# Order of VectorE's masks and evictions in a two-layer graph attention kernel

One layer of graph convolution and one of masked attention run over 32 graphs on one core. The change reorders work: in each full period one softmax mask goes behind an eviction of q; the first period gets a matmul piece between two scores, a later place for the combinations of one weight, another order of its statistics, and other banks for turning h; the last period inverts its softmax sums ahead of an eviction.

## The chip, the core and the metric

The kernel runs on one core of a Trainium2 chip. The core has TensorE (PE in the profile: matmuls and transposes, into PSUM), VectorE (DVE), ScalarE (ACT), GpSimd (POOL), SyncE (SP, which issues transfers here) and DMA engines. [...] The metric is the device time of a whole execution in microseconds (us).

## The reference, cut to what matters

```python
def layer0(x, adj, W, b):            # x: (32, 512, 512) f32, adj: (512, 512) of 0 and 1
    Wi, Wj = W[:, :512], W[:, 512:]
    a, deg = adj.astype(x.dtype), adj.sum(axis=1)
    return deg[None, :, None] * (x @ Wi.T + b) + einsum('ij,bjo->bio', a, x @ Wj.T)

def layer1(h, adj, Wq, bq, Wk, bk, Wv, bv, Wo, bo):       # 8 heads of 64
    q, k, v = split_heads(h @ Wq.T + bq), split_heads(h @ Wk.T + bk), split_heads(h @ Wv.T + bv)
    scores = where(adj == 0, -inf, q @ k^T / 8)
    return merge_heads(softmax(scores) @ v) @ Wo.T + bo

x = layernorm(x + layer0(x, adj, ...))
x = layernorm(x + layer1(x, adj, ...))
```

## The kernel before

The kernel is one software pipeline over the graphs. In period n the attention of graph n-1 (scores, exponential, mask, values, sums) is interleaved with the projections of graph n and, from n = 2, with the output projection of graph n-2. Period 0 has no attention yet, period 1 has no output projection yet, and the last one (32) has no next graph.

Each 512x512x512 product is done in seven products of half the size in each dimension ("pieces" 1 to 7) with sums and differences of quarters, which GpSimd forms for the activations (`combos`) and which are formed once for the weights (`combine`). A piece is 8 matmuls of 128x128 by 256 columns (16 in layer 0, "l0", which has two products). Pieces of one group share a PSUM bank and accumulate in it; there are two such banks, `mma` and `mmb`, which swap roles from one graph to the next.

```python
GROUP = {1: "X", 2: "X", 6: "Y", 7: "Y", 4: "Y", 5: "Z", 3: "Z"}
ORDER = (1, 2, 6, 7, 4, 5, 3)
LATE = (5, 3, 6, 7, 4)

def piece(kind, b, i, bank):
    ...                                             # cut: which quarters; weights come through a ring of transfers
            nc.tensor.matmul(pm[:, c * Q:(c + 1) * Q], lhs, rhs, start=first, stop=..., skip_group_check=True)   # L436
    prefetch()
    if i == 1:
        nc.scalar.copy(p1, pm)                      # L443
    if kind in ("l0", "pj"):
        ...                                         # cut: i == 1 adds p1 on GpSimd (L451)
            nc.vector.tensor_tensor(d, d, pm, op=OP.add)                         # L454
    else:
        ...                                         # cut: v is evicted on L463 and L465
        if i != 2 and not new:
            nc.vector.tensor_tensor(d, pm, d, op=OP.add)                         # L474
            return
        for c in range(2):
            if i == 2:
                nc.scalar.activation(d[:, c], pm[:, c, :], AF.Identity, bias=bc, scale=1.0)
            else:                                   # q's and k's eviction, with bias and p1: L481
                nc.vector.scalar_tensor_tensor(d[:, c], pm[:, c, :], bc, p1[:, c, :], op0=OP.add, op1=OP.add)
```

The attention of a pair of heads: the scores of 128 keys go to one of two `sc` tiles (two banks each), ScalarE takes the exponential in place, VectorE multiplies by the 0/1 mask into an `e` tile, TensorE forms the values and, at the end of a group g of four heads, the sums. `rest` inverts the sums and scales the values.

```python
def scores(b, hp, kc):
    ps = sc_tile()
    for s in range(2):
        nc.tensor.matmul(ps[:, s, :], KT[...], QT[...], start=True, stop=True)    # L490
    nc.scalar.activation(ps, ps, AF.Exp, scale=QSCALE)                            # L494
def mask(hp, kc):
    nc.vector.tensor_tensor(e, ps, edge[...], op=OP.mult)                         # L499
def presum(i, kc):            # kc == 1: GpSimd, L505; kc > 1: VectorE, L507
def values(b, g, kc):         # TensorE into two ov banks, L516
def sums(g, ...):             # TensorE into an sc tile, L526
def drain(b, g):              # ScalarE, L531
def rest(b, g):               # invert x4 (L535), scale x2 (L544), tell (L539), all VectorE
    return [(invert, g, c) for c in range(4)] + [(scale, b, g, 0), (scale, b, g, 1), (tell, b, g)]
```

Layer norm: `stats` measures two 128-row tiles on VectorE (L298, L299) and has three small steps on GpSimd (L300 to L302), `apply` normalizes them on ScalarE (L305). From graph 2 on, h is turned by a trip through memory; in the first periods TensorE turns it (`l0_norm`).

```python
def l0_norm(b, ic):
    y = XT[b][:, ic, :]
    if ic == 0:
        HT[b] = big()
    pt = turn_tile()                                # an sc tile
    for dc in range(DC):
        nc.tensor.transpose(pt[:, dc * P:(dc + 1) * P], y[:, dc * P:(dc + 1) * P], ident)               # L362
    nc.scalar.copy(HT[b][:, :, ic * P:(ic + 1) * P], pt.rearrange("p (c i) -> p c i", c=DC))            # L363
```

The list of a period's work (phases b and c of graph n, then phase a of graph n+1) is cut into steps by its matmul time. The main loop weaves it into the attention, two steps at a time (`size`), one at a time in the last period (`alone`):

```python
for step in range(0, STEPS, size):
    g, kc = divmod(step, NC)
    extra = []
    for i in range(2):
        scores(b, 2 * g + i, kc)
    for f in due:
        values(*f)
    for i in range(2):
        mask(2 * g + i, kc)
    ...
    if due and due[-1][2] == NC - 1:
        ...
        sums(...); drain(pb, pg)
        extra = rest(pb, pg)
    ...
    if alone:
        ...
    else:
        for i in range(2):
            scores(b, 2 * g + i, kc + 1)
        ...
        late = [(mask, 2 * g + i, kc + 1) for i in range(2)] + extra[-1:] + [f for f in late if f[2] > kc]
        for f in extra[:-1] if extra else late[:1]:
            f[0](*f[1:])
        late, extra = late[0 if extra else 1:], []
    for f in todo:                                  # the pieces of this step, and what goes with them
        ...
        run(f)
        some = 0 if f[0] == 0.0 else ... max(1, round(f[0] / PC))
        ...
        if some:                                    # behind a piece: one late operation
            for g in late[:1] + extra[:some]:
                g[0](*g[1:])
            late, extra = late[1:], extra[some:]
    for g in late + extra:
        g[0](*g[1:])
```

The work of period 1 comes from the first branches of `phase_b` and `phase_c`, which are in the diff below. `combine` for wo is five VectorE operations of 128x512 between SBUF tiles (L261 to L263, L269, L270) and seven stores.

Of the kernel before, what the change touches and what calls it, by code (L numbers as in the profile page):

```python
# [25 lines left out]
def gnn_attention_kernel(  # L26
# [36 lines left out]
    nc = tc.nc  # L63
    B, N, D = x.shape
    NC = N // P
# [17 lines left out]
    def big():  # L83
        return work([P, 4, N], "big", 6)

    def mm_tile(bank):
        return psum.tile([P, 512], FT, name="mm" + bank, bufs=1)
# [4 lines left out]
    def sc_tile():  # L92
        return psum.tile([P, 2, N], FT, name="sc", bufs=2)

    def turn_tile():


        return sc_tile()[:, 0, :]
# [4 lines left out]
    TX, TA, TH, TO = {}, {}, {}, {}  # L103
# [56 lines left out]
    def load_wo():  # L160
        t = work([P, NC, D], "xh", 3)
        for h in range(4):
            for g in range(2):
                nc.sync.dma_start(t[32 * h:32 * h + 32, 2 * g:2 * g + 2], woT.rearrange("(g h r d) o -> g h d r o", g=2, h=4, r=2)[g, h])
        return t

    wo = load_wo()
# [185 lines left out]
            y = XT[b][:, ic, :]  # L353
            nc.vector.scalar_tensor_tensor(y, b0_r, deg_c[:, ic:ic + 1], y, op0=OP.mult, op1=OP.add)

    def l0_norm(b, ic):
        y = XT[b][:, ic, :]
        if ic == 0:
            HT[b] = big()
        pt = turn_tile()  # L360
        for dc in range(DC):
            nc.tensor.transpose(pt[:, dc * P:(dc + 1) * P], y[:, dc * P:(dc + 1) * P], ident)  # L362
        nc.scalar.copy(HT[b][:, :, ic * P:(ic + 1) * P], pt.rearrange("p (c i) -> p c i", c=DC))  # L363
# [26 lines left out]
    def quarter(src, j, n):  # L390
        return src[:, 2 * j:2 * j + 2, Q * n:Q * n + Q]
# [104 lines left out]
    def mask(hp, kc):  # L496
        ps = SC.pop(hp)
        e = E[hp % 2, kc] = work([P, 2, N], "e", 4)
        nc.vector.tensor_tensor(e, ps, edge[:, kc:kc + 1, :].to_broadcast([P, 2, N]), op=OP.mult)  # L499
# [28 lines left out]
    def drain(b, g):  # L528

        j = 2 * (b * 2 + g)  # L530
        nc.scalar.activation(RL[g][1], RL[g][0], AF.Identity, accum_out=told[:, j:j + 1])  # L531
# [22 lines left out]
    PC, TR, GA = 1.73, 0.44, 1.9  # L554
    FLUSH = (0.0, None)

    def z(f, *a):
        return (0.0, f, *a)

    def pc(kind, b, i, bank):  # L560
        return (2 * PC if kind == "l0" else PC, piece, kind, b, i, bank)
# [5 lines left out]
    def banks(n):  # L567

        return ("a", "b") if n % 2 == 0 else ("b", "a")
# [46 lines left out]
    def project(m, i):  # L616

        res = [pc("pj", m, i, banks(m)[1])]
        if i == 1:
            res = [z(combos, TO, m, ot_quarter(m), (1,))] + res  # L620
        if i == 2:
            res = [FLUSH] + res + [z(combos, TO, m, ot_quarter(m), (2, 3, 4))]
        return res

    def phase_b(n):

        m = n - 2
        if m < 0:
            res = []
            side = [z(add_bo, 0, i) for i in range(2)]  # L630
            A, K = banks(n)
            for i, bank in ((2, A), (6, K), (5, A), (7, K), (4, K), (3, A)):
                res.append(pc("l0", n, i, bank))
                if i == 4:
                    res += [z(stats, n, 0)]
                if i in (2, 6):
                    res += [z(combine, "wo", nc.vector, int(i == 6))]
                res += side[:1]
                side = side[1:]
            return res + [z(apply, n, 0), z(stats, n, 1), (TR, l0_norm, n, 0), (TR, l0_norm, n, 1)]  # L640
        A = banks(n)[0]
        l0 = {i: pc("l0", n, i, A) for i in ORDER}
        return [l0[2], *project(m, 1), l0[6], *project(m, 2), l0[7], z(add_bo, n - 1, 0), *project(m, 6), l0[4], z(stats, n, 0),
                *project(m, 7), z(between, apply, n, 0), z(between, h_store, n, 0), z(h_load, n, 0), l0[5], z(add_bo, n - 1, 1), *project(m, 4),
                z(h_turn, n, 0), l0[3], z(stats, n, 1), *project(m, 5)]

    def phase_c(n):

        m = n - 2
        norm = [(TR, l0_norm, n, ic) for ic in range(NC)]  # L650
        h = lambda j, i: quarter(HT[n], j, i)
        A, K = banks(n)
        v, q, k = [{i: pc(kind, n, i, bank) for i in ORDER} for kind, bank in (("v", A), ("q", K), ("k", A))]
        if m < 0:
            res = [v[1]] + ([z(apply, n, 1)] if n else []) + [q[1], v[2], norm[2], norm[3], z(combos, TH, n, h, (1, 2)), k[1],
                                                             z(combos, TH, n, h, (3, 4)), q[2], k[2]]
        else:
            res = [v[1], *project(m, 3), z(apply, n, 1), z(h_store, n, 1), z(stats, m, 0), v[2], z(stats, m, 1),
                   q[1], z(h_load, n, 1), k[1], z(apply, m, 0), q[2], z(between, h_turn, n, 1), z(apply, m, 1), z(store, m),
                   z(combos, TH, n, h, (1, 2)), z(combos, TH, n, h, (3, 4)), k[2]]  # L660
        side = []
        if n == 0:

            side = [z(graph_forms, 2), None, z(graph_forms, 0), None, z(graph_forms, 1)]
        for i in LATE:
            for f in q[i], v[i]:
                res += [f] + [g for g in side[:1] if g]
                side = side[1:]
                if i in (6, 7) and n < B - 1:
                    res += [z(load_xa, n + 1, 2 * (i == 7) + (f is v[i]))]  # L670
            if i == 3 and 0 < n < B - 1:
                res += [z(load_x, n + 1)]
            if i == 7 and n + 1 < B:
                res += [z(ahead, n + 1)]
        return res
# [37 lines left out]
    def run(f):  # L713
        f[1](*f[2:])
# [42 lines left out]
    for n in range(1, B):  # L757
        todo = phase_b(n) + phase_c(n) + phase_a(n + 1)
# [16 lines left out]
    due = []  # L775
    for n in range(1, B + 1):
        b = n - 1

        alone = b == B - 1
        size = 1 if alone else 2  # L780
# [9 lines that stand above are left out]
            todo = [f for todo in PERIODS[n][step:step + size] for f in todo]  # L790
            while todo and todo[0][1] is between:
                run(todo.pop(0))
            if due and due[-1][2] == NC - 1:
                pb, pg = due[-1][:2]
                sums(pg, *(((1, 3), 3) if pb == B - 1 else ()))
                drain(pb, pg)
                extra = rest(pb, pg)
            due = [(b, g, kc + i) for i in range(size)]
            late = [(presum, i, c) for _, _, c in due if c > 0 for i in range(2)]
            if alone:  # L800
                if kc > 2 - g:

                    late = []
            else:
                for i in range(2):
                    scores(b, 2 * g + i, kc + 1)
                for f in late if kc > 0 else []:

                    if f[2] == kc:
                        f[0](*f[1:])  # L810
                late = [(mask, 2 * g + i, kc + 1) for i in range(2)] + extra[-1:] + [f for f in late if f[2] > kc]

                for f in extra[:-1] if extra else late[:1]:
                    f[0](*f[1:])
                late, extra = late[0 if extra else 1:], []
            for f in todo:
                if f is FLUSH:
                    some = len(extra)
                else:
                    if f[1] is l0_norm:  # L820

                        for g in late:
                            g[0](*g[1:])
                        late = []
                    run(f)

                    some = 0 if f[0] == 0.0 else len(extra) if step == 0 and alone else max(1, round(f[0] / PC))
                    if f[1] is piece and f[2] == "l0" and f[4] == 3:

                        some = 0  # L830
                if some:
                    for g in late[:1] + extra[:some]:
                        g[0](*g[1:])
# [3 lines that stand above are left out]
# [21 lines left out]
    with tc.If(flag > 0), tc.tile_pool(name="general", bufs=1) as pools.work:  # L858
        wi, wj, wv, wq, wk, wo = [load_w(work([P, DC, D], f"w{i}", 1), src, nc.sync)
                                  for i, src in enumerate((wiT, wjT, wvT, wqT, wkT, woT))]  # L860
# [28 lines left out]
        with tc.For_i(0, B, 1) as b:  # L889
            g = "general"  # L890
# [21 lines left out]
            for hp in range(HP):  # L912
# [6 lines left out]
                for qb in range(NC):  # L919
# [16 lines left out]
                    for s in range(2):  # L936
                        nc.vector.tensor_scalar(pr[:, s, :], pr[:, s, :], sm[:, 6 + s:7 + s], None, op0=OP.mult)
                        pt = mm_tile("b")
# [57 lines left out]
```

## Time and profile before

| | |
|---|---|
| device time, median of 3 (lowest, highest) | 3677.21 us (3675.18, 3678.22) |
| span of the profiled execution | 3673.2 us, 49737 instructions |
| mean granted TensorE clock | 0.999 |
| TensorE matmuls | 3632.5 us busy, 99% of the span |
| TensorE weight loads (overlapping) | 2519.6 us, 69% |
| VectorE, GpSimd, ScalarE | 2375.0, 2005.7, 1034.5 us busy (65%, 55%, 28%) |
| transfers | 530.02 MB, mean 144 GB/s |
| q's and k's eviction (L481), one of two halves | about 0.476 us |
| a mask (L499) | 1.218 us |

How to read it: a busy time is the share of the span in which an engine has an instruction under way. A wait is idle time of an engine just before an instruction, put down to the instruction that released it. In timeline rows the columns are start, duration, engine, line, operation, output and inputs, the number of like instructions merged in the row, and in square brackets idle time before it with its releaser. The rows of TensorE (PE) overlap a little[...].

### The profile page before, as it was taken

The page shows a single profiled execution, that of the slowest core. Times are in us where ns is not written, and L with a number is a line of the kernel's source. Part 1 is how long each engine was busy: PE and PEld are TensorE (multiplying, and loading weights), DVE is VectorE, ACT ScalarE, POOL GpSimd, SP SyncE. Part 2 cuts the span into 40 slices and gives each one's busy share as a digit, 9 for nine tenths or more (in the row PEclk, how much of TensorE's full clock was granted, in tenths as well). Part 3 has the DMA queues.
Part 4 walks back from the last instruction along what each step waited for, and adds up shares of the span by engine and source line. Part 5 has one row for each costly group of instructions (what it writes and reads, how often), then busy time and mean ns, then how long its engine had stood idle before and what let it go on. Part 6 is the DMA issues. An engine that isn't in the chain of part 4 may idle for free.

```text
span 3673.2 us, 49737 instructions
## 1 busy us (share of the span) xinstructions
PE 3632.5 (99%) x18470; PEld 2519.6 (69%) x18470; DVE 2375.0 (65%) x3133; ACT 1034.5 (28%) x1485; POOL 2005.7 (55%) x1984
## 2 busy tenths in 40 slices
PE   9999999999999999999999999999999999999998
PEld 6666776677667766776677677767776777677663
DVE  4666665666666667666666666666666666666665
ACT  2222222222322223222222232232222322222322
POOL 3556545556446564465654565644656445565443
PEclk9999999999999999999999999999999999999999
DMA  8444555455554555655455545555454555455541
GB/s 258 124 126 134 145 160 151 128 144 146 153 158 135 139 137 145 162 152 132 133 148 157 158 123 143 144 149 161 139 139 137 146 158 153 129 140 145 158 133 52
DMA packets 797174, 530.02 MB, mean 144 GB/s; under 512 B 530432, under 2 KB 611840, under 8 KB 796928
## 3 DMA queue, kind: packets, MB, share of 16 engines
q1 hardware_dynamic: 780384, 494.78, 49.9%
q10 hardware_dynamic: 16320, 31.46, 2.4%
q8 instruction: 150, 2.46, 0.3%
q14 instruction: 96, 0.79, 0.1%
q0 software_dynamic: 224, 0.53, 0.0%
HBM read 453.25 MB, written 73.40 MB: 143 GB/s over the span
## 4 chain that ended last, share of the span: by engine, by line
PE 79%; DVE 8%; DMA 2%; issue 1%; POOL 1%; SPq 1%; ACT 0%; DVEq 0%; POOLq 0%
PE mmb L436 26%; PE mma L436 26%; PE sc L490 11%; PE ov L516 10%; PE mmb L334 3%; PE mma L334 3%; DVE rl L535 3%; DVE e L499 2%; DVE oT L544 1%; DMA xa<-hd 1%; DMA hd<-xh 1%; DVE big L382 1%; PE sc L526 1%; DVE q L481 1%; SPq L376 1%
## 5 line engine op out<-in xcount | busy, mean ns | idle before, releaser
L499 DVE TENSOR_TENSOR e<-sc,edge 128x1024 f32<-128x1024 f32 x512 | 607.7, 1218 | 493.2 <-PE ov L516 479.5
L494 ACT ACTIVATE sc<-sc 128x1024 f32<-128x1024 f32 x512 | 494.5, 1007 | 949.5 <-PE sc L490 937.8
L436 PE MATMUL mmb<-ring,big 128*128 128x256 f32 x3144 | 728.4, 380 | 0.0
L436 PE MATMUL mma<-ring,big 128*128 128x256 f32 x3112 | 721.4, 380 | 3.2 <-DVE xh L454 2.5
L436 PEld LDWEIGHTS mmb<-ring,big 128*128 128x128 f32 x3144 | 593.1, 190 | 105.6 <-issue 24.3
L436 PEld LDWEIGHTS mma<-ring,big 128*128 128x128 f32 x3112 | 586.8, 190 | 109.3 <-issue 23.3
L405 POOL TENSOR_TENSOR big<-big 128x512 f32<-128x512 f32 x376 | 489.2, 1327 | 251.3 <-PE sc L490 234.4
L490 PE MATMUL sc<-q,k 64*128 64x512 f32 x2048 | 513.0, 619 | 2.1 <-DVE e L499 2.0
L204 POOL TENSOR_TENSOR xlo<-xh,xhi 128x512 fp32r<-128x512 f32 x128 | 162.3, 1278 | 570.7 <-ACT xhi L203 570.7
L516 PE MATMUL ov<-e,v 128*32 128x512 f32 x4096 | 468.5, 597 | 2.9 <-DVE oT L544 2.9
L436 PE MATMUL mma<-big,ring 128*128 128x256 f32 x1808 | 430.5, 381 | 6.2 <-DVE q L481 5.3
L436 PE MATMUL mmb<-big,ring 128*128 128x256 f32 x1776 | 422.8, 381 | 6.6 <-DVE q L481 5.0
L436 PEld LDWEIGHTS mma<-big,ring 128*128 128x128 f32 x1808 | 340.2, 190 | 72.6 <-issue 14.1
L436 PEld LDWEIGHTS mmb<-big,ring 128*128 128x128 f32 x1776 | 334.3, 190 | 71.4 <-issue 12.2
L490 PEld LDWEIGHTS sc<-q,k 64*128 64x128 f32 x2048 | 165.5, 185 | 287.0 <-DVE e L499 146.2
L300 POOL TENSOR_SCALAR mv<-mv 128x1 f32<-128x1 f32 x256 | 79.8, 312 | 515.8 <-DVE mv L299 503.5
L516 PEld LDWEIGHTS ov<-e,v 128*32 128x32 f32 x4096 | 119.9, 110 | 330.9 <-issue 325.8
L505 POOL TENSOR_TENSOR es<-e 128x1024 f32<-128x1024 f32 x128 | 300.8, 2361 | 51.2 <-DVE e L499 51.2
L507 DVE TENSOR_TENSOR es<-es,e 128x1024 f32<-128x1024 f32 x250 | 300.8, 1224 | 0.0
L451 POOL TENSOR_TENSOR xh<-xh,p 128x512 f32<-128x512 f32 x186 | 230.6, 1268 | 110.3 <-ACT p L443 110.3
L349 POOL TENSOR_TENSOR big<-big,deg_r 128x512 f32<-128x512 f32 x124 | 212.2, 1711 | 76.4 <-DVE big L348 76.4
L454 DVE TENSOR_TENSOR xh<-xh,mmb 128x512 f32<-128x512 f32 x186 | 127.0, 683 | 192.0 <-PE mmb L436 175.2
(157 smaller groups left out, 3549.8 us busy)
## 6 DMA issues: line engine op xcount, KB each, us to landing
ring<-wo SPq DMA_DIRECT2D x217, 256.0 KB, 2.9
ring<-wq SPq DMA_DIRECT2D x160, 256.0 KB, 3.7
ring<-wv SPq DMA_DIRECT2D x160, 256.0 KB, 3.0
ring<-wk SPq DMA_DIRECT2D x160, 256.0 KB, 4.4
ring<-wi SPq DMA_DIRECT2D x155, 256.0 KB, 2.7
ring<-wj SPq DMA_DIRECT2D x155, 256.0 KB, 2.7
xh<-in_x_dram SPq DMA_DIRECT2D x32, 1024.0 KB, 5.5
xa<-in_x_dram SPq DMA_DIRECT2D x124, 256.0 KB, 4.5
```

The costliest lines, as they stand in the source:

```text
L204: nc.gpsimd.tensor_sub(lo, xs, hi.bitcast(FT))
L334: nc.tensor.matmul(pm, parts[w][:, jc, :], adjR[:, jc, :], start=(w == 0 and jc == 0), stop=(w == 1 and jc == NC - 1))
L349: nc.gpsimd.tensor_tensor(XD[b][:, dc, :], XD[b][:, dc, :], deg_r, op=OP.mult)
L405: nc.gpsimd.tensor_tensor(dst, p, q, op=OP.subtract)
L436: nc.tensor.matmul(pm[:, c * Q:(c + 1) * Q], lhs, rhs, start=first, stop=(kc == 1 and n == len(terms) - 1), skip_group_check=True)
L451: nc.gpsimd.tensor_tensor(d, d, p1, op=OP.add)
L490: nc.tensor.matmul(ps[:, s, :], KT[b, hp // 2][r, hp % 2, kc * P:(kc + 1) * P], QT[b, hp // 2][r, hp % 2, :], start=True, stop=True)
L494: nc.scalar.activation(ps, ps, AF.Exp, scale=QSCALE)
L499: nc.vector.tensor_tensor(e, ps, edge[:, kc:kc + 1, :].to_broadcast([P, 2, N]), op=OP.mult)
L505: nc.gpsimd.tensor_add(ES[i], E[i, 0], E[i, 1])
L507: nc.vector.tensor_add(ES[i], ES[i], E[i, kc])
L516: nc.tensor.matmul(PV[g][r][32 * h:32 * h + 32, :], V[b][:, kc, c0:c0 + 32], E[h // 2, kc][:, h % 2, :], start=(kc == 0), stop=(kc == NC - 1))
```

## The change

In every full period the step at which the second group of heads begins (g = 1, kc = 0) now leaves out the late operation behind its first piece, so that the mask that stood there goes behind the second piece, and so behind q's eviction. In the first attention step of all, where there are no values yet to form, a piece is run between the two pairs of scores. Period 1 takes its l0 pieces in another order, measures the second half of the rows first, turns the first half of h in the banks of the pieces rather than in those of the scores, and moves wo's combinations behind pieces of k and q. In the last period, the inversions of the first group's sums are run as soon as the sums are drained, ahead of the next piece.

```diff
-    def l0_norm(b, ic):
+    def l0_norm(b, ic, bank=None):
...
-        pt = turn_tile()
+        pt = mm_tile(bank) if bank else turn_tile()
...
@@ phase_b, period 1
-            for i, bank in ((2, A), (6, K), (5, A), (7, K), (4, K), (3, A)):
+            for i, bank in ((2, A), (6, K), (5, A), (7, K), (3, A), (4, K)):
                 res.append(pc("l0", n, i, bank))
-                if i == 4:
-                    res += [z(stats, n, 0)]
-                if i in (2, 6):
-                    res += [z(combine, "wo", nc.vector, int(i == 6))]
+                if i == 3:
+                    res += [z(stats, n, 1)]
                 res += side[:1]
                 side = side[1:]
-            return res + [z(apply, n, 0), z(stats, n, 1), (TR, l0_norm, n, 0), (TR, l0_norm, n, 1)]
+            return res + [z(apply, n, 1), z(stats, n, 0), z(apply, n, 0), (TR, l0_norm, n, 0, A), (TR, l0_norm, n, 1, K)]
@@ phase_c, periods 0 and 1
-            res = [v[1]] + ([z(apply, n, 1)] if n else []) + [q[1], v[2], norm[2], norm[3], z(combos, TH, n, h, (1, 2)), k[1],
-                                                             z(combos, TH, n, h, (3, 4)), q[2], k[2]]
+            wo = [z(combine, "wo", nc.vector, i) for i in range(2)] if n == 1 else []
+            res = [v[1], q[1], v[2], norm[2], norm[3], z(combos, TH, n, h, (1, 2)), k[1], *wo[:1], z(combos, TH, n, h, (3, 4)), q[2], *wo[1:], k[2]]
@@ main loop, behind the first pair of masks
+            if not due:
+
+                run(todo.pop(0))
@@ last period
+                if g == 1 and kc == 0:
+
+                    for f in extra[:-1]:
+                        f[0](*f[1:])
+                    extra = extra[-1:]
+                hold = False
@@ full periods
-                late, extra = late[0 if extra else 1:], []
+                late, extra, hold = late[0 if extra else 1:], [], bool(extra) and g == 1
             for f in todo:
...
-                    if f[1] is l0_norm:
-
-                        for g in late:
-                            g[0](*g[1:])
-                        late = []
                     run(f)
...
+                    if some and hold:
+
+                        some, hold = 0, False
                 if some:
                     for g in late[:1] + extra[:some]:
```

More of the change, by code (lines that the diff above doesn't have):

```diff
@@ L649, in phase_c @@
         m = n - 2
-        norm = [(TR, l0_norm, n, ic) for ic in range(NC)]
         h = lambda j, i: quarter(HT[n], j, i)
         A, K = banks(n)
+        norm = {ic: (TR, l0_norm, n, ic) for ic in (2, 3)}
         v, q, k = [{i: pc(kind, n, i, bank) for i in ORDER} for kind, bank in (("v", A), ("q", K), ("k", A))]
         if m < 0:
-            res = [v[1]] + ([z(apply, n, 1)] if n else []) + [q[1], v[2], norm[2], norm[3], z(combos, TH, n, h, (1, 2)), k[1],
-                                                             z(combos, TH, n, h, (3, 4)), q[2], k[2]]
+            wo = [z(combine, "wo", nc.vector, i) for i in range(2)] if n == 1 else []
+            res = [v[1], q[1], v[2], norm[2], norm[3], z(combos, TH, n, h, (1, 2)), k[1], *wo[:1], z(combos, TH, n, h, (3, 4)), q[2], *wo[1:], k[2]]
         else:
```

## The prediction

> **What bounds the kernel now.** I read the busy line of the page first, then TensorE's own waits, then the timeline around each kind of wait. From the page:
>
> ```profile
> PE 3632.5 (99%) x18470; PEld 2519.6 (69%) x18470; DVE 2375.0 (65%) x3133; ACT 1034.5 (28%) x1485; POOL 2005.7 (55%) x1984
> ```
>
> TensorE is busy for 3632.5 of the span's 3673.2 us, so at most 40.7 us of idle time are there to be won, 1.1%. The change removes no matmul. It is therefore about TensorE's waits, listed here as waiting line, releaser, total us, times, longest us:
>
> ```profile
> PE mma L436 <- DVE q L481: 5.3, 15, 0.4
> PE mmb L436 <- DVE q L481: 5.0, 14, 0.4
> PE ov L516 <- DVE oT L544: 2.9, 1, 2.9
> PE mma L436 <- DVE xh L454: 2.5, 2, 1.2
> PE sc L362 <- DVE e L499: 2.4, 1, 2.4
> PE sc L490 <- DVE e L499: 2.0, 2, 1.5
> ...
> PE mma L436 <- issue: 0.9, 1, 0.9
> ```
>
> The first two rows are one small wait in nearly every one of the 30 full periods n = 2 to 31; the others occur once or twice, at the start or the end. The timeline of one such period (start us, us, engine, line, ...):
>
> ```profile
> 509.53 1.29 DVE L544 TENSOR_TENSOR oT<-ov,rl 128x512 f32<-128x512 f32 x2
> ...
> 510.55 1.89 PE L436 MATMUL mma<-ring,big 128*128 128x256 f32 x8
> 510.74 1.22 DVE L499 TENSOR_TENSOR e<-sc,edge 128x1024 f32<-128x1024 f32 x1
> ...
> 511.87 0.87 DVE L481 SCALAR_TENSOR_TENSOR q<-mmb,bq_c,p 128x256 f32<-128x256 f32 x2
> ...
> 512.65 1.22 DVE L499 TENSOR_TENSOR e<-sc,edge 128x1024 f32<-128x1024 f32 x1
> 512.79 1.99 PE L436 MATMUL mmb<-big,ring 128*128 128x256 f32 x8 [0.35 <-DVE q L481]
> ...
> 514.62 1.89 PE L436 MATMUL mma<-ring,big 128*128 128x256 f32 x8
> ...
> 516.35 1.89 PE L436 MATMUL mmb<-big,ring 128*128 128x256 f32 x8
> ```
>
> Piece 5 of q is finished on TensorE at about 510.7, but VectorE takes a mask first (510.74) and evicts q only at 511.87; piece 3 of q, which accumulates in the same bank, must wait for that.
>
> [...] the eviction's data lie ready for 1.1 us behind the mask. [...] the last small GpSimd step of a norm, 0.26 us elsewhere, took 1.94 us from 149.16 to 151.10, over two presums of VectorE that ended at about 151.04.
>
> **Part 1, the mask behind q's eviction (periods 2 to 31).** The built order of VectorE differs in a full period in this only: before "oT, oT, mask, q's eviction, mask, v's, told, q's"; after "oT, oT, q's eviction, mask, v's, mask, q's, told". Nothing is added. The eviction can then run from 510.74 to 511.61. TensorE wants the bank 1.73 us (steady distance of two pieces, 514.62 to 516.35) after 510.55, at 512.28: slack 0.67 us, so this wait goes. The gain is more than 0.35 us[...]: 510.55 to 516.35 is 5.80 us where three pieces take 3 x 1.73 = 5.19, a loss of 0.61. Two more periods give 0.60 and 0.61. 30 x 0.61 = 18.3 us, or 17.7 if only the 29 listed waits exist: I take 18.
>
> Does the moved mask hurt the next bank? Mask 511.52 to 512.74; v's eviction (0.68) to 513.4; second mask to 514.6; q's second eviction, two of 0.44, to 515.4. TensorE wants q's bank again at 512.28 + 2 x 1.73 = 515.74, so 0.3 us of slack remain. The score banks freed by these masks are next needed at 526.80, and GpSimd's presum, which starts 0.7 us later, is followed by nothing before 523.39. In period 1 the step begins with q's piece 3, and VectorE has inversions, scaling and then q's eviction without a mask ahead; its wait, the row "issue" of 0.9, stays.
>
> **Part 2, the first period.** Before: from 106.70 the second scores wait 1.51 us for a mask, two l0 pieces wait 1.25 and 1.24 us for VectorE, which wo's combinations hold from 117.88 to 127.8, and then the turning of h waits:
>
> ```profile
> 141.81 2.02 PE L490 MATMUL sc<-q,k 64*128 64x512 f32 x8
> ...
> 144.84 1.22 DVE L499 TENSOR_TENSOR e<-sc,edge 128x1024 f32<-128x1024 f32 x1
> 145.97 0.68 DVE L298 BATCH_NORM_STATS2 st<-xh 128x6 f32<-128x512 f32 x1
> 146.20 0.63 PE L362 MATMUL sc<-ident,xh 128*128 128x128 f32 x4 [2.36 <-DVE e L499]
> ...
> 148.00 1.97 PE L436 MATMUL mmb<-ring,big 128*128 128x256 f32 x8
> ```
>
> After: scores 106.70 to 108.6, a piece to 112.2, scores to 114.1, five pieces of 3.45 us each to 131.4. Every bank is evicted in time by my count (piece 6 evicted at 118.5, wanted at 121.0). The third scores thus start at 131.4 instead of 136.33: 4.9 us won.
>
> But the statistics that h's first half needs are moved. Before, half 0 was measured at 133.77, inside the previous step. After, half 1 is measured there, and half 0 behind a mask of the next step, at the place of the row 145.97, which is 9.64 us after that step's first scores. From there: two statistics (0.9 us each), GpSimd's three small steps, ScalarE's normalization (0.82) per tile. By the same offsets the first tile is normalized about 12.7 us after the step's start and can be turned; the second one's last GpSimd step again meets the presums, now followed at once by wo's combinations, and ends 14.8 to 15.5 us after the start. ScalarE normalizes (0.8) and copies h (0.6), and v's first piece starts at 16.2 to 17.0. So 131.4 + 16.6 = 148.0, where before it started at 148.00. The score banks are no longer what the turn waits for, but the normalization is: TensorE would stand from about 138.9 on, and the 4.9 us are given back. I put this part at 0, give or take 3.
>
> wo's combinations fall where VectorE was idle before: 10.34 us ahead of q's eviction at 161.38. They take 3.1 us undisturbed (one of 0.42 and four near 0.69, as at 47.8 to 56.5) and up to 9 under contention, and are needed only by the next batch's projections.
>
> **Part 3, the last period.**
>
> ```profile
> 3625.80 0.69 DVE L454 TENSOR_TENSOR xh<-xh,mmb 128x512 f32<-128x512 f32 x1 [3.22 <-PE mmb L436]
> 3626.41 3.38 DVE L535 RECIPROCAL rl<-rl 128x128 f32<-128x128 f32 x4
> ...
> 3629.82 1.29 DVE L544 TENSOR_TENSOR oT<-ov,rl 128x512 f32<-128x512 f32 x2
> 3630.57 3.62 PE L516 MATMUL ov<-e,v 128*32 128x512 f32 x16 [2.89 <-DVE oT L544]
> ```
>
> After, the inversions stand ahead of that eviction and start when ScalarE has drained the sums, at 3624.59 + 0.05. They end 1.77 us earlier, and so does the scaling that releases the values: 1.8 us of 2.89 won, 1.1 us stay.
>
> **Sum.** 18 + 0 + 1.8 = 19.8 us: 3677.2 - 19.8 = 3657.4 us, 0.54% faster.
>
> **Rivals.** First, the wait moves: q's second eviction or v's comes late for its bank. For it speaks the slack of only 0.3 us; against it, that VectorE has caught up by the row after. If each period loses 0.3 us again, part 1 brings 9 us and the time is about 3666. Second, the first period really wins its waits: if the statistics were done early enough, the 4.9 us would stay, and the time would be about 3652. For it speaks that the change was built for that; against it, VectorE's order as built. Third, the long one: wo's combinations hold the GpSimd step through all five operations, and the first period loses another 3 us: about 3660. A bound by transfers I leave out: no ring transfer shows among TensorE's waits, and the change adds none, it only issues wo's stores later.
>
> **Range and chances.** Part 1 is the bulk and is well read (17 to 18.5); the first period brings 3 either way, the last 1 to 2.5; the runs before lie within 3 us. 3651 to 3666 should hold it 8 times in 10. 2% is 73.5 us, more than all of TensorE's idle time, so faster by that much is all but excluded; slower by it would need an effect in every period of 2.4 us.
>
> **What would show it.** The rows "DVE q L481" should be gone from TensorE's waits, and TensorE's total idle time should fall from 40.7 to about 30[...]. In the first period a wait of the turn L362 for ScalarE or GpSimd of some 5 us and a second of some 2 us should stand in place of four smaller ones; if none is there, part 2 is wrong and the time nearer 3652. The wait for oT should be about 1.1 us. If the wait of L436 comes back under another releaser in each period, the first rival holds.

## The result and the profile after

The changed kernel takes 3658.03 us (median of 4 runs, 3657.91 to 3658.31), the kernel before on the same chip 3676.19 us (median of 4, 3674.04 to 3678.22). The ratio is 0.9951, 95% interval [0.9934, 0.9968]: 18 us or half a per cent less, with 12 to 24 us inside the interval. The forecast was 3657.4 us in a range of 3651 to 3666.

The busy line of the changed kernel's page:

```profile
PE 3625.8 (99%) x18470; PEld 2527.7 (69%) x18470; DVE 2369.8 (65%) x3133; ACT 1035.5 (28%) x1485; POOL 2003.7 (55%) x1984
```

The number of matmuls is the same. TensorE's idle time is now 3656.2 - 3625.8 = 30.4 us instead of 40.7. Its busy time fell by 6.7 us although it does the same work: at each of the small waits 0.61 us were lost where 0.35 us are listed as idle, so the other 0.26 us are counted as busy (the expectations below call them a refill). In the period that the prediction shows, the piece that waited started 0.51 us late (510.55 to 512.79 is 2.24 us, against 1.73), and took 0.10 us longer to the start of the next (512.79 to 514.62 is 1.83). TensorE's waits in the changed kernel, with the columns waiting line, releaser, total us, times, longest us:

```profile
PE sc L178 <- DVE big L172: 5.6, 3, 4.0
PE mmb L362 <- ACT xh L305: 5.2, 1, 5.2
PE sc L490 <- DVE e L499: 2.4, 2, 1.7
PE mma L362 <- ACT xh L305: 1.8, 1, 1.8
PE mmb L436 <- DVE k L474: 1.5, 1, 1.5
PE ov L516 <- DVE oT L544: 1.2, 1, 1.2
...
PE mma L436 <- issue: 0.8, 1, 0.8
```

The first row is the start of the program (5.7 us before). The two rows for q's eviction (L481), 10.3 us in 29 waits before, are gone. The rows for L454 and for the masks ahead of L362 are gone too, and two waits for the normalization of h (L305) stand in their place. The same step of the same period as before, in the timeline of the changed kernel (start us, us, engine, line, ...):

```profile
510.25 1.29 DVE L544 TENSOR_TENSOR oT<-ov,rl 128x512 f32<-128x512 f32 x2
...
511.50 0.88 DVE L481 SCALAR_TENSOR_TENSOR q<-mmb,bq_c,p 128x256 f32<-128x256 f32 x2
512.29 1.21 DVE L499 TENSOR_TENSOR e<-sc,edge 128x1024 f32<-128x1024 f32 x1
513.02 1.89 PE L436 MATMUL mmb<-big,ring 128*128 128x256 f32 x8
...
515.15 0.86 DVE L481 SCALAR_TENSOR_TENSOR q<-mmb,bq_c,p 128x256 f32<-128x256 f32 x2
...
516.47 1.89 PE L436 MATMUL mmb<-big,ring 128*128 128x256 f32 x8
```

The eviction now stands directly behind the scaling and ends at 512.38, before TensorE wants the bank at 513.02; the row has no wait. The second eviction of q ends at 516.01, 0.46 us before its bank is wanted at 516.47, so that one isn't late either.

The first period, in the timeline of the changed kernel:

```profile
131.44 1.99 PE L490 MATMUL sc<-q,k 64*128 64x512 f32 x8
...
143.29 0.81 ACT L305 ACTIVATE xh<-xh,mv 128x512 f32<-128x512 f32 x1 [1.85 <-POOL mv L302]
...
144.16 1.12 PE L362 MATMUL mmb<-ident,xh 128*128 128x128 f32 x4 [5.21 <-ACT xh L305]
144.26 1.94 POOL L302 TENSOR_SCALAR mv<-mv 128x1 f32<-128x1 f32 x1
...
147.10 1.12 PE L362 MATMUL mma<-ident,xh 128*128 128x128 f32 x4 [1.83 <-ACT xh L305]
...
148.01 3.62 PE L436 MATMUL mmb<-ring,big 128*128 128x256 f32 x8
151.43 2.20 PE L436 MATMUL mma<-big,ring 128*128 128x256 f32 x8
```

The third scores start at 131.44 (136.33 before), and v's first piece at 148.01, just where it started before. But this piece then takes 3.42 us to the next one's start; before it took 1.81 (148.00 to 149.81). The engine table by stretches says why. Its columns are the stretch, its length, then busy time and number of instructions of TensorE, weight loads, VectorE, ScalarE and GpSimd, then TensorE's granted clock, the share of the DMA engines and GB/s:

```profile
132.00:138.80 6.80, 6.80 (x48) 1.90 (x44) 3.69 (x4) 2.62 (x3) 0.26 (x1) 1.00 0.25 73
138.80:144.00 5.20, 0.15 (x2) 0.00 (x0) 5.13 (x9) 3.35 (x5) 1.58 (x5) 0.79 0.01 2
144.00:147.20 3.20, 1.21 (x5) 0.82 (x6) 3.17 (x4) 1.07 (x3) 2.10 (x2) 0.50 0.00 0
147.20:151.40 4.20, 4.20 (x12) 3.51 (x13) 1.91 (x4) 0.90 (x2) 0.00 (x0) 0.50 0.00 0
151.40:155.00 3.60, 3.60 (x17) 3.12 (x16) 0.00 (x0) 1.17 (x2) 0.00 (x0) 0.91 0.32 87
```

During the long wait the granted clock falls to a half: it is 1.00 up to 141, 0.90 over 141 to 142 and 0.50 from 142 to 151.40. The mean of 0.91 over the last 3.60 us means about 0.65 us more at a half, so it is full again at about 152 (0.50 over 151.40 to 152.00, 0.98 over 152 to 153). A 128x256 matmul has a duration of 634 ns in this piece and 379 ns at the same place before.

The last period, changed kernel, timeline:

```profile
3613.24 1.92 PE L516 MATMUL ov<-e,v 128*32 128x512 f32 x16 [1.18 <-DVE oT L544]
...
3623.58 2.34 POOL L505 TENSOR_TENSOR es<-e 128x1024 f32<-128x1024 f32 x1
...
3625.95 2.36 DVE L499 TENSOR_TENSOR e<-sc,edge 128x1024 f32<-128x1024 f32 x2 [3.72 <-POOL es L505]
3627.23 1.13 PE L490 MATMUL sc<-q,k 64*128 64x512 f32 x4 [1.69 <-DVE e L499]
```

The wait for the scaled values is 1.18 us (2.89 before), and the 16 matmuls behind it span 1.92 us; before they spanned 3.62, at a granted clock of 0.54 (columns as in the table above):

```profile
3630.50:3634.20 3.70, 3.63 (x17) 0.69 (x17) 3.70 (x6) 0.00 (x0) 1.29 (x1) 0.54 0.00 0
```

On the other hand the scores now wait 1.69 us for masks, which wait for a presum on GpSimd; TensorE did not have this wait before. The same place in the kernel before:

```profile
3640.31 2.37 POOL L505 TENSOR_TENSOR es<-e 128x1024 f32<-128x1024 f32 x1
...
3642.72 1.22 DVE L499 TENSOR_TENSOR e<-sc,edge 128x1024 f32<-128x1024 f32 x1 [1.46 <-POOL es L505]
...
3643.44 1.99 PE L490 MATMUL sc<-q,k 64*128 64x512 f32 x8
```

A mask waited for that presum before, too, and in both kernels the presum stands in GpSimd's queue behind the small steps of the statistics. But it ended at 3642.68, 20.74 us after the sums of the first group (3621.94), and TensorE came to these scores at 3643.44, 21.50 us after the sums. Now TensorE comes 18.09 us after the sums (3606.32), 3.4 us earlier, and the presum ends 19.60 us after them, only 1.1 us earlier: of the 1.7 us that the scaling is earlier, 0.6 goes to the eviction of L454, which ran ahead of the inversions before (3625.80) and now runs between the scaling and the masks (3613.70).

Marks in the timeline divide the program: the first scores of period 1, the second scores of its third step (where the second group of heads begins), and the sums of the first and of the second group in the last period. Between them the three parts can be read off separately, in us:

| stretch | before | after | gain |
|---|---|---|---|
| period 1: first scores to the second group's second scores | 106.70 to 169.28: 62.58 | 106.49 to 171.22: 64.73 | -2.15 |
| full periods: from there to the sums near the end | to 3621.94: 3452.66 | to 3606.32: 3435.10 | 17.56 |
| last period: from there to the next group's sums | to 3647.09: 25.15 | to 3630.03: 23.71 | 1.44 |
| sum | | | 16.85 |

The profiled spans differ by 17.0 us, the medians by 18.2.

### The profile page after: what moved, and what is told of

Its sections match the earlier page's. It is cut to its first block, busy times and chain, and to the rows that moved or that the text cites. A ratio compares the mean times of both kernels' runs of the same rounds, so it can differ in the third digit from the quotient of the medians.

```text
span 3656.2 us, 49768 instructions
## 1 busy us (share of the span) xinstructions
PE 3625.8 (99%) x18470; PEld 2527.7 (69%) x18470; DVE 2369.8 (65%) x3133; ACT 1035.5 (28%) x1485; POOL 2003.7 (55%) x1984
## 4 chain that ended last, share of the span: by engine, by line
PE 97%; DVE 1%; POOL 1%; issue 0%; ACT 0%; DMA 0%; SPq 0%; DVEq 0%; POOLq 0%
PE mma L436 31%; PE mmb L436 31%; PE sc L490 13%; PE ov L516 12%; PE mmb L334 4%; PE mma L334 3%; PE sc L526 2%; PE mmb L607 0%; PE mma L607 0%; DVE e L499 0%; POOL es L505 0%; DVE es L507 0%; DVE rl L535 0%; PE sc L735 0%; DMA big<-in_adj_dram 0%
## 5 line engine op out<-in xcount | busy, mean ns | idle before, releaser
L454 DVE TENSOR_TENSOR xh<-xh,mma 128x512 f32<-128x512 f32 x186 | 126.9, 682 | 191.2 <-PE mma L436 174.6
```

## The experiments

**The mask alone.** The kernel before, with the hold and nothing else:

```diff
-                late, extra = late[0 if extra else 1:], []
+                late, extra, hold = late[0 if extra else 1:], [], bool(extra) and g == 1
...
+                    if some and not alone and hold:
+                        some, hold = 0, False
```

> The kernel before with the mask put behind q's eviction in the full periods and nothing else. My theory (the mask is nearly the whole gain): all rows of TensorE waiting for q's eviction go, 30 x 0.6 us are won, 3676 - 18 = 3658 us, so as fast as the whole change. Rival (the three parts share the gain, and the mask alone gives the 10 us of its listed waits): 3666 us.

Measured: 3657.17 us against 3675.24 us before, ratio 0.9950 [0.9933, 0.9966]. All rows for q's eviction are gone, all other waits of the kernel before are still there (2.9 us for the scaling, 2.5 for L454, 2.4 for the turn). Its list begins:

```profile
PE sc L178 <- DVE big L172: 5.5, 3, 4.1
PE ov L516 <- DVE oT L544: 2.9, 1, 2.9
PE mma L436 <- DVE xh L454: 2.5, 2, 1.2
```

The mask gives the whole gain. A gain of the listed waits alone, 10 us, would have been 3665: the 0.26 us that are not listed count too.

**The first period alone.** The changed kernel with `hold` always false and without the inversions of the last period:

```diff
-                late, extra, hold = late[0 if extra else 1:], [], bool(extra) and g == 1
+                late, extra, hold = late[0 if extra else 1:], [], False
...
-                if g == 1 and kc == 0:
-                    for f in extra[:-1]:
-                        f[0](*f[1:])
-                    extra = extra[-1:]
```

> The kernel before with the change of the first period alone. My theory from the two traces: 4.9 us are won up to the third scores, then TensorE stands 5.2 and 1.8 us for the normalization of h and runs at half its clock for some 8 us, so the part as a whole loses about 2 us: 3678 us, and the scores of the second group start about 2 us later than before. Rival (the part is neutral, as predicted): 3676 us, no shift.

Measured: 3676.62 us against 3675.24, ratio 1.0003 [0.9994, 1.0012]. The time alone can't tell 2 us from none. The trace can: first scores at 106.33, the second group's second scores at 171.09, 64.76 us where the kernel before takes 62.58. The part loses 2.2 us, as in the changed kernel.

**The last period alone.** The kernel before with the inversions ahead of the piece:

```diff
+                if g == 1 and kc == 0:
+                    for f in extra[:-1]:
+                        f[0](*f[1:])
+                    extra = extra[-1:]
```

> The kernel before with the earlier inversions of the last period alone. My theory: the wait for the scaled values falls from 2.9 to 1.2 us, the values behind it run at full clock (1.9 instead of 3.6 us), and a new wait of some 1.7 us for a mask that GpSimd's presum holds back takes about half of that again: about 1.5 us won, 3674.5 us; the trace decides, not the time. Rival: the new wait belongs to another part of the change and is absent here, 3.4 us won.

Measured: 3676.18 us against 3675.24, ratio 1.0001 [0.9993, 1.001], not to be told apart by time. In the trace the sums are 23.72 us apart (3621.03 to 3644.75; 25.15 before), the wait for the scaling is 1.18 us and the new wait for a mask is there with 1.70 us. So the new wait belongs to this part; 1.4 us stay.

**Two masks ahead of the eviction.** The changed kernel, with the suspected cost doubled:

```diff
                     if some and hold:
-                        some, hold = 0, False
+                        for g in late[:1]:
+                            g[0](*g[1:])
+                        late, hold = late[1:], False
```

> The changed kernel with both masks ahead of q's eviction in the full periods, twice as many as the kernel before had. If the eviction's place in VectorE's queue sets the wait, the eviction ends 1.13 us later than in the kernel before and TensorE waits 0.35 + 1.13 = 1.5 us in 30 periods, with a refill of 0.26 us each: 3658 + 30 x 1.74 = 3710 us. Rival (the step has slack elsewhere that takes up the delay, so that the wait doesn't grow with the delay): below 3690 us.

Measured: 3712.36 us, ratio to the kernel before 1.010 [1.008, 1.012]. Its waits of TensorE:

```profile
PE mma L436 <- DVE q L481: 22.3, 15, 1.5
PE mmb L436 <- DVE q L481: 22.1, 15, 1.5
```

30 waits of 1.48 us, as expected from 0.35 + 1.13, and 54.3 us more than the changed kernel, 1.81 for each (1.74 expected). With none, one and two masks ahead of the eviction the listed wait is 0, 0.35 and 1.48 us: the eviction's place in VectorE's queue sets it, and the step has no slack beyond the 0.64 us seen above (512.38 to 513.02).

**The wait filled.** Is it the standing that costs the clock? The changed kernel with five idle matmuls into the bank of the turn, whose results are overwritten:

```diff
         pt = mm_tile(bank) if bank else turn_tile()
+        if bank and ic == 0:
+            for _ in range(5):
+                nc.tensor.matmul(pt, ident, deg_r, start=True, stop=True)
```

> The changed kernel with five idle matmuls (128x128 by 512, about 0.86 us each, their results overwritten) into the bank in which h is about to be turned, so that TensorE is busy during most of its 5.2 us wait. The waits for the normalization end when they did. If the half clock after the wait comes from TensorE's having stood, the granted clock stays at 1.0, v's first piece takes 1.8 instead of 3.4 us, and about 2 us are won: 3656 us. Rival (the slow piece has another cause, a transfer or a copy of h): the piece keeps its 3.4 us, 3658 us or more.

Measured: 3655.33 us (0.9945 [0.9932, 0.9959]), 2.7 us less than the changed kernel by the medians. Intervals some 10 us wide can't tell differences of a few us apart; here and below such differences rest on the traces. (The five show as x10, two instructions for each matmul of the program, and what was called 8 matmuls of a piece above are four of the program. The 0.86 us of the expectation were an estimate: eight instructions of 128x512 on L607 take 3.43 us in the kernel before, from 25.44 to the next at 28.87, so two take 0.86. The five took 4.56 us from 138.33, 0.91 each.) The same stretches, with the same columns (this execution runs 0.5 us ahead of the one above, so they lie 0.5 us later in the program):

```profile
138.80:144.00 5.20, 4.47 (x14) 1.91 (x12) 5.13 (x8) 2.90 (x4) 2.03 (x6) 1.00 0.00 0
144.00:147.20 3.20, 0.91 (x8) 0.63 (x7) 3.13 (x5) 1.28 (x2) 1.66 (x1) 1.00 0.00 0
147.20:151.40 4.20, 4.20 (x21) 3.62 (x21) 1.40 (x3) 1.73 (x3) 0.00 (x0) 1.00 0.19 62
```

The clock is 1.00 throughout, v's first piece takes 1.81 us to the next (147.05 to 148.86), and 21 matmuls stand where 12 did. Useless work makes the kernel faster here. From the first scores to the second group's second ones it takes 62.40 us (105.94 to 168.34), 2.33 less than the changed kernel: the half clock is all of the 2.15 us by which the first period had lost. The two waits for the normalization end as before, 37.67 and 40.62 us after the first scores (37.67 and 40.61 in the changed kernel). With the same copies of h and the same transfers the slow piece is gone once TensorE doesn't stand, so neither of these was the cause.

**The statistics earlier.** The changed kernel, period 1 in the old order of pieces, half 0 measured inside the first step and normalized ahead of the next exponentials, half 1 measured ahead of the next masks (`between` is the loop's mark for that place):

```diff
-            for i, bank in ((2, A), (6, K), (5, A), (7, K), (3, A), (4, K)):
+            for i, bank in ((2, A), (6, K), (5, A), (7, K), (4, K), (3, A)):
...
-                if i == 3:
-                    res += [z(stats, n, 1)]
+                if i == 4:
+                    res += [z(stats, n, 0)]
...
-            return res + [z(apply, n, 1), z(stats, n, 0), z(apply, n, 0), (TR, l0_norm, n, 0, A), (TR, l0_norm, n, 1, K)]
+            return res + [z(between, apply, n, 0), z(between, stats, n, 1), (TR, l0_norm, n, 0, A), (TR, l0_norm, n, 1, K)]
@@ phase_c: behind v[1]
+            ([z(apply, n, 1)] if n else [])
```

> The changed kernel with the l0 pieces of period 1 in the order of the kernel before, so that the first half of the rows is measured inside the first step and normalized ahead of the next exponentials, and the second half is measured ahead of the next masks. My theory (the chain of statistics, GpSimd and normalization gave back what the first period had won): no wait of the turn over 0.5 us, the clock stays at 1.0, the second group's scores start some 10 us earlier than in the changed kernel: 3648 us. Rival (another wait takes the place, for the banks or for the other half): less than 5 us won, above 3653 us.

Measured: 3649.26 us, ratio 0.9926 [0.9912, 0.9939], 8.8 us less than the changed kernel. Its timeline:

```profile
135.70 1.51 ACT L305 ACTIVATE xh<-xh,mv 128x512 f32<-128x512 f32 x2
...
138.19 2.02 PE L490 MATMUL sc<-q,k 64*128 64x512 f32 x8
...
140.15 0.66 PE L362 MATMUL mmb<-ident,xh 128*128 128x128 f32 x4
...
141.85 1.99 PE L436 MATMUL mmb<-ring,big 128*128 128x256 f32 x8 [0.61 <-ACT big L363]
```

Half 0 is normalized by 137.2, before TensorE is there, and v's first piece starts at 141.85 instead of 148.01. The stretch from the first scores to the second group's second ones is 56.46 us (106.70 to 163.16), 8.3 less than in the changed kernel. A short wait of 0.8 us for L454 came with the old order of pieces, and one of 0.6 us for the copy of h remains; their 1.4 us are most of the 1.7 us that my 10 us were too many.

**The last wait, a miss.** The changed kernel with the statistics of the last graph but one a step later, so that GpSimd forms both presums ahead of their small steps:

```diff
-[own[0], z(stats, m, 0), z(stats, m, 1)], [own[1], z(apply, m, 0), z(apply, m, 1), z(store, m)], []]
+[own[0]], [own[1], z(stats, m, 0), z(stats, m, 1), z(apply, m, 0), z(apply, m, 1), z(store, m)], []]
```

> The changed kernel with the last-but-one graph's statistics one step later in the last period, so that GpSimd takes both presums ahead of their small steps. If the new wait of scores for a mask comes from the presum queued behind those steps, it goes: 1.7 us and a refill won, 3656 us. Rival (statistics now stand in VectorE's way in the next step): no gain or a loss of 1 to 2 us, 3658 to 3660 us.

Measured: 3662.24 us (0.9963 [0.9949, 0.9976]), 4.2 us more than the changed kernel. The wait of 1.69 us is gone (the 0.7 us that scores still wait for a mask is another wait, which the changed kernel has too, 0.74 us at 3602.38). But its timeline has a new one:

```profile
3629.56 0.81 ACT L305 ACTIVATE xh<-xh,mv 128x512 f32<-128x512 f32 x1 [0.46 <-POOL mv L302]
3630.28 1.91 ACT L494 ACTIVATE sc<-sc 128x1024 f32<-128x1024 f32 x2
...
3632.68 1.07 PE L526 MATMUL sc<-es,ones 128*32 128x512 f32 x8 [4.20 <-DVE e L499]
```

The scores of 3624.65 were long done. ScalarE took four normalizations first, each waiting for GpSimd, and the exponentials stood behind them until 3630.28. TensorE waited 4.20 us and had a clock of 0.68 over the next 5.4 us. The rival had named VectorE; it was ScalarE's queue.

**The normalization behind the exponentials.** The same, with `apply` and `store` one step later again:

```diff
-[own[0], z(stats, m, 0), z(stats, m, 1)], [own[1], z(apply, m, 0), z(apply, m, 1), z(store, m)], []]
+[own[0]], [own[1], z(stats, m, 0), z(stats, m, 1)], [z(apply, m, 0), z(apply, m, 1), z(store, m)]]
```

> The changed kernel with the last-but-one graph's statistics one step later, as in the edit that lost 4 us, and its normalization still one step later, behind the last exponentials. If that loss came from ScalarE's queue (the normalization, waiting for GpSimd, held back two exponentials, so that TensorE stood 4.2 us and then ran at half its clock), it goes, and the wait of scores for a mask stays away too: 3656 us, 2 us less than the changed kernel. Rival (the statistics themselves are in VectorE's way): 3658 us or more.

Measured: 3656.60 us (0.9942 [0.9928, 0.9955]), 1.4 us less than the changed kernel by the medians; in the trace the two sums are 21.76 us apart (3606.61 to 3628.37; 23.71 in the changed kernel), 1.95 less. Both waits are gone; only the 0.7 us of that other wait stay.

**Both ends.** The earlier statistics were combined with each of the two last edits:

> Both of the last two edits on the changed kernel. They touch different ends of the program, so the gains should add: 3646 us if both theories hold.

Measured: 3654.38 us (0.9940 [0.9927, 0.9954]): 3649.3 plus the 4.2 of the miss would be 3653.5. The edits add, the expectation fell with its second theory.

> That edit together with the earlier statistics in the first period. The two touch different ends of the program: 3649.3 - 2 = 3647 us.

Measured: 3648.21 us, ratio 0.9920 [0.9906, 0.9933], 29.6 us less than the kernel before in the same runs (3677.80) and the fastest of all. Its profiled span is 3645.8 us, the one with the earlier statistics alone 3647.9; by their intervals the two can't be told apart.

## Why the prediction was right, and where it was right by cancellation

- **Part 1, 18 us: right.** 17.56 us in the full periods, 0.585 for each of 30, and 18.1 by the mask-only kernel. Both halves of the estimate held: the wait goes, and its price was 0.61 us where 0.35 is listed. The slack forecast for q's second eviction was 0.3 us, measured 0.46. The first rival, the wait moving to the next bank, fell.
- **The wait of the row "issue" stays: right,** 0.85 us in both traces.
- **Part 2, 0 give or take 3: the size was off by 2.15 us.** The chain held step by step: third scores at 131.4 (131.44), waits of about 5 and 2 us (5.21 and 1.83), v's first piece at 148.0 (148.01), GpSimd's last step 1.94 us long (from 144.26, beside VectorE's presums from 143.80; the same step before it took 0.26). The third rival fell: wo's combinations took 3.1 us (146.07 to 149.15) and began only as that step ended; in the kernel before, where GpSimd was busy for 9.62 of the 9.90 us beside them, the five took 9.39 us in sum (117.88 to 127.78). What the sum lacked is the price of standing: a half clock until about 152, worth 2.2 to 2.3 us. TensorE stood from 138.95 to 144.16; the clock fell within this wait of 5.21 us, at about 142, and was full again some 5 us after TensorE had taken up steady work at 147.10. The second rival (3652 if the statistics came early) named the right lever: the kernel that does it takes 3649.26.
- **Part 3, 1.8 us: 1.44 measured, by two errors of opposite sign.** The wait fell by 1.71 us as forecast. The values behind it also got their full clock back (593 ns for one of their matmuls, 1061 before), 1.70 us that the sum lacked. And an equal share was lost again to a wait that I hadn't looked for: TensorE came to the next scores 3.4 us earlier, the presum on GpSimd ended only 1.1 us earlier, and a mask and the scores behind it wait, the scores 1.69 us (with that wait gone, in the run with the normalization behind the exponentials, the stretch was 1.95 us shorter).
- **Idle time:** about 30 forecast, 30.4 measured.

The total of 19.8 us was 17 to 18 in fact. Part 1 carries it; the two ends are small, and their missed terms happened to cancel in part. That the time itself came within 0.6 us of the forecast is luck, too: the kernel before took 1.0 us less beside the changed one (3676.19) than the 3677.2 from which the forecast started.

## What to carry to other kernels

Where one engine is busy 99% of the time, look at the whole price of each short repeated wait: the distance of starts against the steady distance gives it (0.61 us where 0.35 was listed), and the order of two operations in the releaser's queue may be all of it. A long single wait can cost more than its length: with the one of 5.21 us here the half clock cost 2.2 to 2.3 us more. Count the slow matmuls behind such a wait, and try to fill it if it can't be removed (five idle matmuls won those 2.3 us back). When a wait goes, ask what the engine meets next and what stands ahead of that in another engine's order of instructions. In three places here an operation with its data ready stood behind earlier ones of the same engine: q's eviction 1.1 us behind a mask, a presum behind small steps (it ended at 3625.92; at 3621.06 with the statistics a step later), and exponentials behind normalizations (until 3630.28, for scores done at 3626.64).

## What the runs showed of the hardware that I had not expected

The granted clock fell around waits of 5.21 us (0.50 from 142 to 152 in the changed kernel), 4.20 us (a mean of 0.68 over the next 5.4 us in the miss above) and 2.89 us (0.54 from 3630.5 to 3634.2 in the kernel before), and not around one of 2.36 us (1.00 from 144.0 to 148.2 in the kernel before). At the half clock a 128x256 matmul took 634 ns instead of 379, and 16 matmuls of 512 columns spanned 3.62 us instead of 1.92. What sets the clock was not shown.

Waits of the same length had different prices. With the mask alone the wait of 2.88 us was as long as in the kernel before, but the 16 matmuls behind it spanned 3.14 us, not 3.62:

```profile
3612.72 3.14 PE L516 MATMUL ov<-e,v 128*32 128x512 f32 x16 [2.88 <-DVE oT L544]
```

And where the statistics alone came a step later (the miss above), the clock was 1.00 through the whole wait of 4.20 us and fell only when TensorE worked again:

```profile
3628.00:3632.60 4.60, 0.49 (x8) 0.00 (x0) 1.28 (x2) 3.44 (x4) 1.26 (x4) 1.00 0.28 107
3632.60:3638.00 5.40, 5.32 (x36) 1.90 (x40) 1.07 (x1) 0.00 (x0) 0.00 (x0) 0.68 0.28 103
```

The clock column may miss a slow stretch: at the start of the program, behind a wait of 4.07 us, the 128x128 transposes of L178 took 421 ns each in the kernel before, as long as those of L362 at the half clock in the changed kernel (273 ns at full clock in the kernel before), while the column reads 1.00 from 0 to 12. Durations of like matmuls are worth a look beside it.
